# Feed-forward of a decoder layer: outputs of the down product with tokens on the partitions, operands exchanged, closing products in a tile of their own

## The chip, the core and the metric

The kernel runs on one core of one Trainium2 chip. A core has a matrix engine (TensorE, "PE" in the profile; its weight loads are listed apart as "PEld"), a vector engine (VectorE, "DVE"), a scalar engine (ScalarE, "ACT"), a general engine (GpSimd, "POOL") and a queue that only issues transfers (SyncE, "SP"). They run side by side and wait for one another through semaphores; 16 DMA engines move the data. SBUF is the working memory with 128 partitions. PSUM, which takes the results of TensorE, has eight banks, each of 512 fp32 per partition.

The metric is the time of one execution on the device, in microseconds (us). Lower is better.

## What is computed

The reference is one decoder layer on `x` of 8 sequences x 256 tokens x 512 features, all in fp32: self-attention, a recurrence that takes the place of cross-attention, and a gated feed-forward, each followed by an addition and a layer norm. Only the last one is touched here:

```python
gate_w = spline_reconstruct(gate_cp, INTER, HIDDEN)     # 2048 x 512
up_w   = spline_reconstruct(up_cp, INTER, HIDDEN)       # 2048 x 512
down_w = spline_reconstruct(down_cp, HIDDEN, INTER)     # 512 x 2048
gate  = jnp.einsum('bsh,ih->bsi', hidden_states, gate_w)
up    = jnp.einsum('bsh,ih->bsi', hidden_states, up_w)
inter = jax.nn.silu(gate) * up
return jnp.einsum('bsi,hi->bsh', inter, down_w)
...
x = _layernorm(x + _L0_ffn_ref(x, ...), axis=-1)
```

The weights are cubic splines through about 8,100 control points each, so most of a row is piecewise cubic. The kernel uses that: the down product is made of an exact part, 16 tiles of 128 intermediate features, of which each quarter of 32 is used for one quarter of the 512 outputs, and of a closing part, in which sums of intermediate features ("fin") stand for all that the exact part leaves out.

## The kernel before

The 2048 tokens are handled in four groups `b` of 512 tokens (`GT`), each of four chunks of 128 (`TC`). Attention comes first and fills the time up to about 402 us. From there the feed-forward runs group after group (loop at L939). Every instruction is issued in program order on its engine: the class `Ordered` (L299 to L312) pins the order that the Python code writes, so what stands earlier in the code stands earlier in each engine's queue. All instructions pass through that class and therefore carry its line, L308, in the profile; groups are told apart by the names of tiles.

One group, in the order of the code:

- `fill(DC)` (L942, groups 1 and 2 only) makes the transposes of the next group's input (`tr_x2`, four PSUM tiles of the pool `ps_mm`, which has four buffers in all). They are copied out alternately by ACT and DVE (L712).
- `gate_up(b, j)` for j = 0 to 7 (L842): two gate products `pg` (in `ps_mm`) and two up products `pu` (in `ps_big`, four buffers), ACT makes `sg = silu(pg)`, DVE `inter = pu * sg`. Right after each, `gather` (L858) sends both `inter` tiles by a transfer from SP's queue into `nat`, 256 KB each, 16 in a group. In groups 1 and 2 the moments of the next group's input (`ps_mom`) come after j = 2.
- `reads` (L953): transfers on SP's queue that bring the next group's input `xg` into place.
- `exact(b, t)` for t = 0 to 15 (L865): the exact down product, four matmuls per t, one for each output quarter d. The stationary operand is the weight `wd` (32 rows x 128 columns), the moving one `inter` (32 rows x 512 tokens). Result: `y0` to `y3`, four tiles of the pool `ps_big`, outputs on the partitions, tokens along the free axis. The four d sit in different 32-row strips of the array.
- After t = 7: the generator `residual(b)` (L920) is queued: POOL copies `x2` into `x2p` (36 copies, permuted features, each for all 512 tokens), handed out six at a time in the slots after t = 8 and later; and `into_sums(b, v)` for v = 0 to 3 (L875): products `ps_s` from `nat`, copied by ACT or DVE to `sum`, and sent by a transfer from POOL's queue into `fin` (`sorted_[b]`). POOL's four transfers stand ahead of its 36 copies.
- `finish(b)` (L894): four closing products (128 rows x 128 columns, 512 tokens moving) are added into `y0` to `y3` in PSUM, then each is copied to SBUF (`ys`), by ACT and DVE in turn.
- `outcome(b, t)` (L907), one generator for each chunk: four transposes `tr_y`, DVE adds `x2p` and sums up (`h3`, `s3`), and `norm_plain` (L366) makes the layer norm: DVE `nm`, ACT Square with sum, POOL `va` and `rs`, DVE the result; then SP sends it to `out`.

A generator in `chains` goes one step further at each call of `slot()`. The four `outcome` generators of group b - 1 are queued in the exact products of group b, behind t = 0 (L957), so their transposes stand between t = 0 and t = 1 of group b, and their transfers to `out` behind all gathers of group b on SP's queue. Those of the last group run behind everything (L973).

An fp32 matmul appears in the profile as two instructions ("passes"), each with its own weight load; a transpose as one.

## Time and profile before

| what | value |
|---|---|
| three runs | 602.85, 604.49, 605.11 us; median 604.49 |
| the profiled execution, its own time | 603.72 us |
| its span, first to last instruction | 601.9 us |
| mean granted clock of TensorE | 0.996 |
| feed-forward | 402.4 to 601.9 us |
| group 0: gates from, exact from, sums end, closing from | 402.4, 424.3, 439.9, 447.1 us |
| group 1 | 452.4, 470.1, 487.7, 495.6 us |
| group 2 | 500.9, 518.6, 536.2, 544.8 us |
| group 3 | 548.4, 562.3, 579.9, 587.1 us |

Group 0 has the last output projections and norms of attention between gates and exact products (416 to 424 us).

The profile names a group of instructions by what is written and read: `y<-inter,wd` are the exact products, `y<-fin,wd` the closing ones, `tr_y<-ident,ys` the transposes of the result, `x2p<-x` POOL's copies, `nat<-inter` the gathers. A line of the timeline has: start in us, length in us of the stretch of like instructions, engine, L308, operation, out<-in, rows*columns and sizes, count, and in brackets the engine's idle time before it with what ended it. Lengths of matmuls are modelled up to the arrival of the last result; the pace of the engine is read from start to start.

### The profile page before, as it was taken

To read this page: it belongs to the slowest core of one execution; us is meant where nothing else is said; L and a number is where in the kernel's file an instruction comes from. 1 tells how busy PE (TensorE), PEld (TensorE's weight loads), DVE (VectorE), ACT (ScalarE), POOL (GpSimd) and SP (SyncE) were. 2 spreads that over 40 slices of the span, in tenths; PEclk is the share of its full clock that TensorE was granted. 3 is DMA by queue.
4 is the path that set the end of the run, shared out by engine and by line. 5 is a ranking of instruction groups with operands and counts; after the bars stand their busy time and mean duration, and the time that the engine had idled before them with its cause. 6 is when DMAs were issued, how large, how long until landed. Compare 5 with 4: busy or idle time off the path is not lost.

```text
span 601.9 us, 9688 instructions
## 1 busy us (share of the span) xinstructions
PE 577.3 (96%) x3346; PEld 292.0 (49%) x3346; DVE 335.5 (56%) x742; ACT 277.9 (46%) x820; POOL 219.3 (36%) x495
## 2 busy tenths in 40 slices
PE   9999999998899999999999999999999999999993
PEld 4544555555455555554554555444444434433432
DVE  0203634658676665886674777776926605714614
ACT  0114643655654554655455667665315404504502
POOL 0000997065544336444340311300272262142244
PEclk9999999999999999999999999999999999999998
DMA  8104253034224115323210564659328986984931
GB/s 294 64 0 157 80 167 114 27 98 144 74 71 141 36 54 175 105 71 96 79 36 2 158 152 102 173 152 216 65 72 223 205 233 179 227 213 134 212 142 70
DMA packets 38961, 75.50 MB, mean 125 GB/s; under 512 B 3937, under 2 KB 8289, under 8 KB 38913
## 3 DMA queue, kind: packets, MB, share of 16 engines
q1 hardware_dynamic: 34576, 62.75, 39.4%
q0 software_dynamic: 3328, 10.96, 5.5%
q10 hardware_dynamic: 1008, 1.18, 0.7%
q8 instruction: 26, 0.43, 0.3%
q14 instruction: 23, 0.18, 0.1%
HBM read 42.86 MB, written 11.04 MB: 90 GB/s over the span
## 4 chain that ended last, share of the span: by engine, by line
PE 82%; DVE 10%; ACT 3%; DMA 2%; issue 2%; POOL 1%; POOLq 0%; DVEq 0%; SPq 0%; ACTq 0%
PE y L308 12%; PE ps_k L308 9%; PE ps_v L308 9%; PE ps_o L308 8%; PE ps_q L308 6%; PE tr_e L308 6%; PE sc L308 5%; PE pg L308 5%; PE ps_s L308 5%; PE av L308 5%; PE pu L308 5%; DVE nmax L308 3%; PE ps_mom L308 2%; ACT e L308 2%; DVE eT L308 2%
## 5 line engine op out<-in xcount | busy, mean ns | idle before, releaser
L308 ACT ACTIVATE e<-sc,nmax 128x256 f32<-128x256 f32 x256 | 120.2, 480 | 102.1 <-DVE nmax L308 102.1
L308 DVE TENSOR_REDUCE nmax<-sc 128x2 f32<-128x512 f32 x128 | 84.5, 682 | 73.6 <-PE sc L308 67.7
L308 POOL TENSOR_TENSOR taps<-taps 128x256 f32<-128x256 f32 (+1 forms) x144 | 89.0, 618 | 33.1 <-DMA taps<-in_down_taps 26.3
L308 PEld LDWEIGHTS tr_e<-ident,e 128*128 128x128 f32 x512 | 56.9, 140 | 25.2 <-issue 22.5
L308 PE MATMUL tr_e<-ident,e 128*128 128x128 f32 x512 | 68.3, 276 | 0.5 <-DVE eT L308 0.4
L308 PE MATMUL y<-inter,wd 32*128 32x512 f32 x512 | 63.0, 598 | 0.0
L308 PE MATMUL ps_o<-w_o,yT 128*128 128x512 f32 x128 | 60.0, 600 | 2.6 <-DVE eT L308 2.3
L308 PE MATMUL ps_k<-xT_g,w_k 128*128 128x512 f32 x128 | 58.8, 601 | 0.6 <-DVE eT L308 0.6
L308 PE MATMUL ps_v<-w_v,xT_g 128*128 128x512 f32 x128 | 58.6, 598 | 0.4 <-DVE eT L308 0.4
L308 PE MATMUL ps_q<-xT_g,w_q 128*128 128x512 f32 x128 | 58.2, 596 | 0.0
L308 POOL TENSOR_SCALAR va<-ss 128x1 f32<-128x1 f32 x32 | 7.3, 227 | 136.8 <-ACT x L308 86.6
L308 POOL TENSOR_TENSOR rs<-va,neghalf 128x1 f32<-128x1 f32 x48 | 28.9, 602 | 69.4 <-DVE va L308 66.7
L308 ACT ACTIVATION_READ_ACCUMULATOR e<-sc,nmax 128x1 f32 x256 | 53.2, 208 | 0.0
L308 DVE TENSOR_TENSOR inter<-pu,sg 128x512 f32<-128x512 f32 x64 | 41.2, 686 | 18.3 <-PE pu L308 9.4
L308 ACT ACTIVATE sg<-pg 128x512 f32<-128x512 f32 x64 | 37.2, 596 | 18.4 <-PE pg L308 18.4
L308 DVE COPY eT<-tr_e 128x512 f32<-128x512 f32 x64 | 43.8, 684 | 0.5 <-PE tr_e L308 0.4
L308 PEld LDWEIGHTS y<-inter,wd 32*128 32x128 f32 x512 | 26.7, 184 | 32.7 <-issue 27.0
L308 PE MATMUL av<-eT,v_g 128*32 128x256 f32 x512 | 36.7, 385 | 5.0 <-ACT eT L308 2.7
L308 ACT COPY eT<-tr_e 128x512 f32<-128x512 f32 x64 | 37.5, 585 | 2.4 <-PE tr_e L308 2.4
L308 POOL TENSOR_TENSOR r<-r 128x1024 f32<-128x1024 f32 x8 | 15.2, 1895 | 63.6 <-DMA r<-in_ctxT 63.6
L308 PE MATMUL sc<-k_g,q_g 32*128 32x256 f32 x512 | 37.4, 401 | 0.2 <-ACT e L308 0.2
L308 PEld LDWEIGHTS ps_o<-w_o,yT 128*128 128x128 f32 x128 | 22.8, 190 | 26.4 <-issue 21.5
(98 smaller groups left out, 737.5 us busy)
## 6 DMA issues: line engine op xcount, KB each, us to landing
nat<-inter SPq DMA_DIRECT2D x64, 256.0 KB
taps<-in_down_taps SPq DMA_DIRECT2D x40, 256.0 KB
taps<-in_up_taps SPq DMA_DIRECT2D x16, 384.0 KB
xg<-xd SPq DMA_DIRECT2D x8, 616.0 KB
r<-in_ctxT SPq DMA_DIRECT2D x8, 512.0 KB
x_t<-in_x SPq DMA_DIRECT2D x16, 256.0 KB
fin<-sum POOLq DMA_DIRECT2D x16, 256.0 KB, 5.1
out<-h SPq DMA_DIRECT2D x16, 256.0 KB
```

The costliest lines, as they stand in the source:

```text
L308: return lambda *a, **k: self.tc.keep_in_program_order(f(*a, **k))
```

## The change

The exact product exchanges its operands: `inter` (32 rows x 128 tokens of one chunk c) is now the stationary one, `wd` (32 rows x 128 outputs) the moving one. For each t there are 16 matmuls of 128 columns in place of four of 512, in the order c, then d. The result `y` has tokens on the partitions. It is one PSUM tile of four banks (bank d holds the four chunks of quarter d), of a new pool `ps_four` with a single buffer, opened when the attention's `ps_big` is closed. The four up products in flight are slices of a tile of the same tag ("big4"), so `y` of a group and `pu` of the next take turns in the same four banks.

The closing product is made apart, with exchanged operands too, per chunk, in a tile `ps_c` of `ps_mm` (16 matmuls of 128 columns in place of four of 512); it is no longer added in PSUM. DVE makes `h3 = y + x2p` from PSUM first and then `h3 = ps_c + h3` with the sum. The transposes `tr_y` and the copies `ys` are gone. Square's unused output goes to a tile `o` in SBUF.

The order changes as well: `finish(b)` issues the first two steps of all four `outcome` generators (the four additions of `y`, then closing products and second additions chunk by chunk), behind the last exact product of the same group. What is left of each, the norm and the transfer to `out`, is queued one chunk at a time behind j = 0, 1, 2, 3 of the next group's `gate_up` (`late_chains`).

```diff
-    ps_big = ctx.enter_context(tc.tile_pool(name="ps_big", bufs=4, space=PSUM))
     ps_mm = ctx.enter_context(tc.tile_pool(name="ps_mm", bufs=4, space=PSUM))
+    scored = ExitStack()
+    ps_big = scored.enter_context(tc.tile_pool(name="ps_big", bufs=4, space=PSUM))
...
+    scored.close()
+    ps_big = ctx.enter_context(tc.tile_pool(name="ps_four", bufs=1, space=PSUM))
...
     def gate_up(b, j):
         pgs, pus = [], []
-        for w, pool, tag, to in ((wg, ps_mm, "mm", pgs), (wu, ps_big, "big", pus)):
+        if not j:
+            ups[b] = ps_big.tile([P, 4, GT], F32, tag="big4", name="pu")
+        for w, to in ((wg, pgs), (wu, pus)):
             for h in range(2):
                 at = slice(h * K2, (h + 1) * K2)
-                ps = pool.tile([P, GT], F32, tag=tag, name="pg" if w is wg else "pu")
+                ps = ps_mm.tile([P, GT], F32, tag="mm", name="pg") if w is wg else ups[b][:, j % 2 * 2 + h, :]
...
     def exact(b, t):
         if t == 0:
-            ys[b] = [ps_big.tile([P, GT], F32, tag="big", name=f"y{d}") for d in range(ND)]
-        for d in range(ND):
-            q = slice(d * 32, (d + 1) * 32)
-            nc.tensor.matmul(
-                ys[b][d], lhsT=wd[q, t * P : (t + 1) * P], rhs=inters[b, t][q, :], start=(t == 0), stop=False
-            )
+            ys[b] = ps_big.tile([P, ND, TC, P], F32, tag="big4", name="y")
+        for c in range(TC):
+            for d in range(ND):
+                q = slice(d * 32, (d + 1) * 32)
+                nc.tensor.matmul(
+                    ys[b][:, d, c, :],
+                    lhsT=inters[b, t][q, c * P : (c + 1) * P],
+                    rhs=wd[q, t * P : (t + 1) * P],
+                    start=(t == 0 and c == 0),
+                    stop=(t == NTILE - 1 and c == TC - 1),
+                )
...
     def finish(b):
-        y = late.tile([P, ND, GT], F32, tag="ys", name="ys")
+        new = [outcome(b, c) for c in range(TC)]
+        for _ in range(2):
+            for chain in new:
+                next(chain)
+        late_chains.extend(new)
+
+    def outcome(b, c):
+        h3 = rows.tile([P, D], F32, tag="row", name="h3")
+        h, x2p = (a.rearrange("p (d o) -> p d o", d=ND) for a in (h3, xps[b][:, c, :]))
+        nc.vector.scalar_tensor_tensor(h, ys[b][:, :, c, :], 1.0, x2p, ALU.mult, ALU.add)
+        yield
+        acc = ps_mm.tile([P, D], F32, tag="mm", name="ps_c")
         for d in range(ND):
             nc.tensor.matmul(
-                ys[b][d],
-                lhsT=wd[:, (NTILE + d) * P : (NTILE + d + 1) * P],
-                rhs=sorted_[b][:, d, :],
-                start=False,
+                acc[:, d * P : (d + 1) * P],
+                lhsT=sorted_[b][:, d, c * P : (c + 1) * P],
+                rhs=wd[:, (NTILE + d) * P : (NTILE + d + 1) * P],
+                start=True,
                 stop=True,
             )
-            (nc.vector.tensor_copy if d % 2 else nc.scalar.copy)(y[:, d, :], ys[b][d])
-        ys[b] = y
-
-    def outcome(b, t):
-
-        tr = ps_mm.tile([P, D], F32, tag="mm", name="tr_y")
-        for d in range(ND):
-            nc.tensor.transpose(tr[:, d * P : (d + 1) * P], ys[b][:, d, t * P : (t + 1) * P], ident)
-        yield
-        h3 = rows.tile([P, D], F32, tag="row", name="h3")
         s3 = small.tile([P, 1], F32, tag="s3", name="s3")
-        nc.vector.scalar_tensor_tensor(h3, tr, 1.0, xps[b][:, t, :], ALU.mult, ALU.add, accum_out=s3)
-        yield from norm_plain(h3, s3, h3, tr)
-        r0 = (b * TC + t) * P
+        nc.vector.scalar_tensor_tensor(h3, acc, 1.0, h3, ALU.mult, ALU.add, accum_out=s3)
+        yield
+        o = work.tile([P, D], F32, tag="o", name="o", bufs=2)
+        yield from norm_plain(h3, s3, h3, o)
+        r0 = (b * TC + c) * P
         nc.sync.dma_start(out=out[r0 : r0 + P, :], in_=h3)
...
             if b:
+                if late_chains:
+                    chains.append(late_chains.pop(0))
                 slot()
...
             exact(b, t)
-            if b and t == 0:
-                chains += [outcome(b - 1, c) for c in range(TC)]
             slot()
...
         assert not units
+        settle()
         finish(b)
-    chains += [outcome(NG - 1, t) for t in range(TC)]
+    chains += late_chains
     settle()
```

More of the change, by code (lines that the diff above doesn't have):

```diff
@@ L839, in decoder_kernel @@
     made[0] = -1e9
-    inters, ys, sorted_, xps, nats = {}, {}, {}, {}, {}
+    inters, ys, sorted_, xps, nats, late_chains, ups = {}, {}, {}, {}, {}, [], {}
     def gate_up(b, j):
         pgs, pus = [], []
-        for w, pool, tag, to in ((wg, ps_mm, "mm", pgs), (wu, ps_big, "big", pus)):
+        if not j:
+            ups[b] = ps_big.tile([P, 4, GT], F32, tag="big4", name="pu")
+        for w, to in ((wg, pgs), (wu, pus)):
             for h in range(2):
                 at = slice(h * K2, (h + 1) * K2)
-                ps = pool.tile([P, GT], F32, tag=tag, name="pg" if w is wg else "pu")
+                ps = ps_mm.tile([P, GT], F32, tag="mm", name="pg") if w is wg else ups[b][:, j % 2 * 2 + h, :]
                 nc.tensor.matmul(ps, lhsT=w[at, j * P : (j + 1) * P], rhs=xgs[b][at, j, :], start=True, stop=True)
@@ L894, in finish @@
     def finish(b):
-        y = late.tile([P, ND, GT], F32, tag="ys", name="ys")
+        new = [outcome(b, c) for c in range(TC)]
[9 more added lines that the diff above has]
+        acc = ps_mm.tile([P, D], F32, tag="mm", name="ps_c")
         for d in range(ND):
             nc.tensor.matmul(
-                ys[b][d],
-                lhsT=wd[:, (NTILE + d) * P : (NTILE + d + 1) * P],
-                rhs=sorted_[b][:, d, :],
-                start=False,
+                acc[:, d * P : (d + 1) * P],
+                lhsT=sorted_[b][:, d, c * P : (c + 1) * P],
+                rhs=wd[:, (NTILE + d) * P : (NTILE + d + 1) * P],
+                start=True,
                 stop=True,
             )
-            (nc.vector.tensor_copy if d % 2 else nc.scalar.copy)(y[:, d, :], ys[b][d])
-        ys[b] = y
-    def outcome(b, t):
-        tr = ps_mm.tile([P, D], F32, tag="mm", name="tr_y")
-        for d in range(ND):
-            nc.tensor.transpose(tr[:, d * P : (d + 1) * P], ys[b][:, d, t * P : (t + 1) * P], ident)
-        yield
-        h3 = rows.tile([P, D], F32, tag="row", name="h3")
-        s3 = small.tile([P, 1], F32, tag="s3", name="s3")
-        nc.vector.scalar_tensor_tensor(h3, tr, 1.0, xps[b][:, t, :], ALU.mult, ALU.add, accum_out=s3)
-        yield from norm_plain(h3, s3, h3, tr)
-        r0 = (b * TC + t) * P
+        s3 = small.tile([P, 1], F32, tag="s3", name="s3")
+        nc.vector.scalar_tensor_tensor(h3, acc, 1.0, h3, ALU.mult, ALU.add, accum_out=s3)
+        yield
+        o = work.tile([P, D], F32, tag="o", name="o", bufs=2)
+        yield from norm_plain(h3, s3, h3, o)
+        r0 = (b * TC + c) * P
         nc.sync.dma_start(out=out[r0 : r0 + P, :], in_=h3)
```

## The prediction

> **What bounds the kernel now.** I read the page first, then the timeline of the last group, whose order all groups share, then the stretches around it for the transfers.

> ```profile
> PE 577.3 (96%) x3346; PEld 292.0 (49%) x3346; DVE 335.5 (56%) x742; ACT 277.9 (46%) x820; POOL 219.3 (36%) x495
> ...
> PE 82%; DVE 10%; ACT 3%; DMA 2%; issue 2%; POOL 1%; POOLq 0%; DVEq 0%; SPq 0%; ACTq 0%
> ```

> TensorE is busy 96% of the span and holds 82% of the chain that ends last. So work taken from it counts, as long as nothing else is close behind. The next two views ask what is close behind in the feed-forward.

> ```profile
> 564.84 1.97 PE L308 MATMUL tr_y<-ident,ys 128*128 128x128 f32 x16
> ...
> 566.74 6.29 PE L308 MATMUL y<-inter,wd 32*128 32x512 f32 x56
> ...
> 572.96 7.09 PE L308 MATMUL ps_s<-nat,sf 128*64 128x512 f32 x32
> ...
> 579.97 7.15 PE L308 MATMUL y<-inter,wd 32*128 32x512 f32 x64
> 580.09 0.69 DVE L308 COPY sum<-ps_s 128x512 f32<-128x512 f32 x1 [2.74 <-PE ps_s L308]
> ...
> 581.08 0.55 POOL L308 DMA_DIRECT2D fin<-sum  x1 [1.28 <-DVE sum L308]
> ...
> 581.62 8.18 POOL L308 COPY x2p<-x 128x4 f32<-128x4 f32 x36
> ...
> 587.05 3.70 PE L308 MATMUL y<-fin,wd 128*128 128x512 f32 x8
> ...
> 592.97 0.69 ACT L308 ACTIVATE tr_y<-h,nm 128x512 f32<-128x512 f32 x1 [2.45 <-DVE nm L308]
> ```

> TensorE goes from the transposes through exact products, sums, exact products and closing without a hole. But POOL's copies to `x2p` end at 589.8, 2.8 us after the last exact product (587.0). They can't start sooner: POOL first issues the four `fin` transfers, and the last waits for DVE's copy of the last sum. Counting from S, the end of the sums (579.9), `x2p` is complete at S+9.9. The copies of all four groups end at S+9.9 (449.8, 497.6, 546.1, 589.8). Today that hurts nobody, since `x2p` is read only behind the transposes.

> ```profile
> 552.00:556.00 4.00, 4.00 (x22) 1.83 (x20) 3.00 (x5) 2.76 (x5) 0.00 (x0) 1.00 0.92 210
> 556.00:560.00 4.00, 4.00 (x20) 1.74 (x18) 3.14 (x6) 2.54 (x5) 0.00 (x0) 1.00 1.08 214
> ...
> 568.00:572.00 4.00, 4.00 (x42) 1.85 (x38) 3.00 (x8) 1.84 (x6) 2.90 (x7) 1.00 1.08 207
> 572.00:575.00 3.00, 3.00 (x22) 0.97 (x16) 0.00 (x0) 0.06 (x1) 0.00 (x0) 1.00 0.95 343
> ```

> The last two columns are the DMA engines' share and GB/s. From 552 to 572 the engines are full at some 211 GB/s: 20 us x 0.211 = 4.2 MB, the 16 gathers of 0.262 MB. Behind them, at 343 GB/s, go the four `out` transfers, which today stand behind all gathers on SP's queue. The last gather's semaphore comes at 572.5. The first sum product that reads it starts at 573.8 (0.86 behind 572.96). So the gathers are only 1.3 us from being the bound.

> **The change, part by part.** Times are relative to G, the start of a group's gates, and to S.

> Exact products. Before, a t takes two passes of 512 columns at 0.429 us from start to start, 0.858 us, the four strips side by side. After, eight passes of 128 columns, each with a weight load of 128 columns in all strips. Nearest rows: `tr_y`, 16 passes of 128 columns with a load each at 0.108 us from start to start; and the full-height fp32 product `ps_wq`, 0.112. So 0.86 to 0.89 us; I take 0.88, +0.2 per half group. This needs 64 instructions per t in 0.88 us, 13.7 ns each. The trace shows no such pace for long: its densest 64 PE instructions (67.64 to 69.41, score products and transposes) come at 27.7 ns. That end is a rival below. I take the fast end, because the loads of the four strips of `y` start within 0.02 us of each other.

> [...]

> First exact product. It needs all four banks that `pu` held, so it waits for the last `inter`; today it already does (470.15 to 472.61 for one t), so 0.

> Transposes. Three times between t = 0 and t = 1: 1.90 plus one change of shape, 0.09: -1.99 each. The fourth set is in the tail.

> Closing. 32 passes at 0.112 = 3.57 us in place of 3.43. What hides the 0.14 is DVE's chain, next.

> The new wait. DVE's first addition reads `x2p` straight behind the exact products, so it starts at S+9.95, not at S+7.3. Then four additions at 0.60 from start to start (as `inter`, same form) and four second additions at 0.74 (`h<-tr_y` less its `nm`): starts at S+12.35, 13.1, 13.8, 14.6. Each `ps_c` buffer of `ps_mm` comes free some 0.7 later, and behind these wait, on TensorE, the next group's transposes and gates. Closing products are done by S+12.6 even where `fin` lands at S+8.5 (groups 1 and 2), so DVE sets the time. Groups 0 and 1: `tr_x` of the second chunk must be copied by DVE behind its last second addition, S+15.3 to 16.0, before `pg` has its two buffers: gates start at S+16.1. Before: 452.43 - 439.88 = 12.55, and 500.91 - 487.74 = 13.15: +3.55 and +2.95. Group 2 has no `tr_x`: two `ps_c` buffers free at S+13.85, before 548.35 - 536.22 = 12.15: +1.7. Last group: the first Square waits for `nm` behind all second additions, S+15.6; before 592.97 - 579.88 = 13.1: +2.5; from there on the rows are as now (4.84 to the last result). `y` is free at S+12.6, before `pu` needs it.

> The moved transfers. The four `out` of a group now go out behind j = 3 to 6 of the next group (two of them in the pause for the moments), ahead of the last two gathers on SP's queue. 1.05 MB at 343 GB/s and 0.95 share: 2.9 us later for the last gather. Below 0 it can't go; at the gathers' rate it would be 5 us. I take 2.9, measured on these very transfers. Group 3: last gather at 572.5 - 548.35 = G+24.15, now G+27.05; its first reader was at G+25.45: +1.6, in place of the -1.8 that TensorE would gain. Groups 1 and 2: packets through at G+25.9, semaphore some 0.4 later, now G+29.2; reader before at G+29.25: 0, in place of -1.8. Moments and `xg` on these queues come later but have 2 us to spare.

> The norms beside the gates: ACT gets a Square each at 0.81, 1.99 for 1.72 us of TensorE at j = 1 to 4; up to 1 us late, and the gathers hide it.

> Sum: group 0 exact +0.2; into group 1 +3.55; group 1 0; into 2 +2.95; group 2 0; into 3 +1.7; group 3 +1.6; tail +2.5. Together +12.5 against the profiled execution's 603.7 (span 601.9 and 1.8 around it): 616.2. The median stands 0.8 above that execution, inside the runs' scatter, so I say 616.

> One more risk: in group 3 TensorE idles about 3.4 us before the last gather. After the last matmul (593.1) the granted clock holds at 0.99 to 596.8 and reads 0.50 behind that; a hole of 2.0 us at 158.6 left it at 1.00. So 3.4 us should just pass; else up to 2 us more, which the range holds.

> [...]

> **Rivals.** (1) The `out` transfers slip between the gathers without delaying them. For: they are written while DMA also waits for `inter`; against: the share is 0.92 and up. Then groups 1 and 2 gain 1.8 each and group 3 1.3: 616.2 - 1.8 - 1.8 - 2.9 = 609.7. (2) The issue of PE instructions becomes the bound at 27.7 ns: 1.77 us per t, +7.3 per half. Group 0 +7.1; the second halves end at S+14.4 and push DVE by 4.6, four times, 18.4; first halves of groups 1 to 3 beyond the gathers 5.4, 5.4 and 3.7: 616.2 + 40 = 656. Against: nothing in the trace is held up by issue for long. (3) `x2p` is not waited for: POOL would have to be done by S+7.1. Gates then lose only 0.85, 0.2 and 0.1 and the tail gains 0.2: +0.2 + 0.95 + 1.6 = 606.4, no measurable change. (4) Faster: TensorE alone stays the bound, at the boundaries and at the sums. It decides where the copies are done by S+7.1 and the gathers by G+23.6. Then three times -1.99, exact +1.4, boundaries and tail +0.95: 600.1. For: 96% busy; against: both margins above, 2.8 and 1.3 us, read from the trace.

> **How the numbers follow.** Forecast 0.64, (1) 0.15, (2) 0.08, (3) 0.07, (4) 0.06. The time is the forecast's, 616. The range, 606 to 624, holds the forecast with its bounds (`out` at the slow rate 6 more in all, the clock 2), (1) and (3), and leaves out (2) and (4). Within 0.5% of 604.5 is 601.5 to 607.5, about what runs of this kernel can tell from no change: faster 0.06, same 0.07, slower 0.87.

> **What would show it.** Right: `tr_y` gone; exact products at 0.86 to 0.89 us per t; DVE idle before the first addition with POOL's `x2p` as releaser, in all four groups; `ps_s` or its second product waiting for the transfer `nat` in group 3; holes on TensorE of 2 to 4 us at each boundary. Wrong: exact products well above 1 us per t; additions that start right behind the exact products; sums that start 1.8 us sooner after G in every group.

## The result, and the profile after

The changed kernel takes 642.0 us (641.33 to 643.1), beside 604.8 for the kernel before on the same chip: ratio 1.0616, 95% interval 1.0595 to 1.0637. The forecast was 616 us, range 606 to 624: the sign was right, the size was not.

The profiled execution took 643.1 us, its span is 641.3. Starts of first instructions, read from the timeline as for the table of before, give the loss by stage. S is the end of the sums, and the last column holds the next group's first gate product, or the end of the span.

| group | gates to sums, before and after | sums | S to next gates or end | loss |
|---|---|---|---|---|
| 0 | 30.55, 36.93 | 6.93, 6.93 | 12.55, 16.03 | 9.9 |
| 1 | 28.39, 38.41 | 6.92, 9.27 | 13.17, 15.45 | 14.7 |
| 2 | 28.39, 32.51 | 6.92, 6.92 | 12.13, 15.92 | 7.9 |
| 3 | 24.61, 29.53 | 6.92, 6.92 | 22.02, 23.88 | 6.8 |

With 0.2 us ahead of 402 us this makes the 39.4 us by which the span grew. The forecast had put 10.7 us of its 12.5 into the fourth column. That column holds 11.4 us of the 39.4; 25.4 lie between gates and sums. The page of the changed kernel says where to look (busy time, the DMA queue of instructions, and three groups with, behind the last bar, TensorE's or DVE's idle time ahead of them):

```profile
PE 584.4 (91%) x4914; PEld 328.5 (51%) x4914; DVE 337.0 (53%) x750; ACT 272.0 (42%) x812; POOL 218.0 (34%) x495
...
q8 instruction: 39, 0.64, 0.4%
...
L308 PE MATMUL y<-wd,inter 32*128 32x128 f32 x2048 | 63.7, 278 | 11.6 <-issue 7.2
...
L308 DVE TENSOR_TENSOR inter<-pu,sg 128x512 f32<-128x512 f32 x64 | 41.2, 686 | 36.7 <-ACT sg L308 23.0
...
L308 PE MATMUL pu<-xg,wu 64*128 64x512 f32 x128 | 36.0, 634 | 15.6 <-DVE inter L308 11.5
```

TensorE is busy 7 us longer than before, not 39. Two waits are new and were in no part of the forecast: up products wait for `inter`, and exact products wait for "issue", which means for nothing that the profile shows. The timeline of group 0's gates shows the first.

```profile
404.69 1.29 DVE L308 TENSOR_TENSOR inter<-pu,sg 128x512 f32<-128x512 f32 x2 [0.82 <-ACT sg L308]
...
406.03 1.13 PE L308 MATMUL pu<-xg,wu 64*128 64x512 f32 x4 [0.59 <-DVE inter L308]
...
407.28 1.29 DVE L308 TENSOR_TENSOR inter<-pu,sg 128x512 f32<-128x512 f32 x2 [1.30 <-PE pu L308]
...
408.62 1.13 PE L308 MATMUL pu<-xg,wu 64*128 64x512 f32 x4 [0.60 <-DVE inter L308]
```

The up products of each j start when DVE has read those of j - 1, and DVE in turn waits for them. One j takes 408.62 - 406.03 = 2.59 us. In the kernel before (here in group 3) it took 557.90 - 556.18 = 1.72, and no up product waited for DVE:

```profile
556.18 1.02 PE L308 MATMUL pu<-xg,wu 64*128 64x512 f32 x4
...
557.29 1.29 DVE L308 TENSOR_TENSOR inter<-pu,sg 128x512 f32<-128x512 f32 x2 [0.43 <-ACT sg L308]
...
557.90 1.02 PE L308 MATMUL pu<-xg,wu 64*128 64x512 f32 x4
```

The up products alternate between two pairs of banks, so the data leave room for two j at a time, but all four banks are one tile. Gates and up products together take 20.0 to 23.9 us in place of 13.9 to 17.6.

The second wait lies in the exact products. This is group 1 in the timeline, and then the same stretch by windows (busy time and count of PE, PEld, DVE, ACT and POOL, then TensorE's granted clock, DMA share and GB/s).

```profile
489.75 5.20 PE L308 MATMUL y<-wd,inter 32*128 32x128 f32 x179
489.77 5.03 SPq L308 DMA_DIRECT2D xg<-xd  x3
...
499.54 1.43 PE L308 MATMUL y<-wd,inter 32*128 32x128 f32 x17 [4.60 <-issue]
```

```profile
494.00:497.00 3.00, 0.94 (x35) 0.75 (x27) 0.00 (x0) 0.00 (x0) 0.00 (x0) 1.00 0.75 148
497.00:500.70 3.70, 1.16 (x17) 1.14 (x17) 0.00 (x0) 0.00 (x0) 0.00 (x0) 0.75 0.73 158
500.70:503.00 2.30, 2.30 (x11) 0.77 (x8) 0.00 (x0) 0.00 (x0) 0.00 (x0) 0.50 0.66 175
503.00:506.00 3.00, 3.00 (x10) 0.83 (x8) 0.00 (x0) 0.59 (x1) 0.49 (x1) 0.56 0.60 135
```

In the middle of products whose data have long been there, TensorE stops for nearly 5 us, with no engine at work and no releaser. Transfers are under way (the gate inputs `xg` of group 2). Afterwards the granted clock is 0.50 (the half clock), and the sums of this group take 9.27 us in place of 6.92. A hole of 2.90 us lies in the second half of group 2 (569.84), again with the half clock behind it (0.50 from 574.0 to 576.9 us).

What the forecast was mostly about did come. This is the view of the tile `x2p` (what ended DVE's idle time before it read the tile, us and times):

```profile
L308 DVE SCALAR_TENSOR_TENSOR h<-y,x2p x16: 680/681/692, 456.4 to 629.2; 128x512 f32<-128x512 f32 x16
its engine sat idle before it (us, times) until:
  POOL x2p L308: 27.2, 3
  PE y L308: 11.3, 1
```

In three groups DVE waits for POOL's copies, as forecast in all four. In group 2 the copies were done first (574.9 us), since its exact products ran into the hole at 569.84.

### The profile page after: what moved, and what is told of

Its sections match the earlier page's. It is cut to its first block, busy times and chain, and to the rows that moved or that the text cites. A ratio compares the mean times of both kernels' runs of the same rounds, so it can differ in the third digit from the quotient of the medians.

```text
span 641.3 us, 12808 instructions
## 1 busy us (share of the span) xinstructions
PE 584.4 (91%) x4914; PEld 328.5 (51%) x4914; DVE 337.0 (53%) x750; ACT 272.0 (42%) x812; POOL 218.0 (34%) x495
## 5 line engine op out<-in xcount | busy, mean ns | idle before, releaser
L308 ACT ACTIVATE e<-sc,nmax 128x256 f32<-128x256 f32 x256 | 120.0, 479 | 102.0 <-DVE nmax L308 102.0
L308 DVE TENSOR_REDUCE nmax<-sc 128x2 f32<-128x512 f32 x128 | 84.5, 682 | 73.6 <-PE sc L308 67.7
L308 POOL TENSOR_TENSOR taps<-taps 128x256 f32<-128x256 f32 (+1 forms) x144 | 89.1, 619 | 32.7 <-DMA taps<-in_down_taps 24.6
L308 PE MATMUL y<-wd,inter 32*128 32x128 f32 x2048 | 63.7, 278 | 11.6 <-issue 7.2
L308 PEld LDWEIGHTS y<-wd,inter 32*128 32x128 f32 x2048 | 60.9, 191 | 19.2 <-issue 11.6
L308 PEld LDWEIGHTS tr_e<-ident,e 128*128 128x128 f32 x512 | 56.9, 141 | 25.2 <-issue 22.5
L308 PE MATMUL tr_e<-ident,e 128*128 128x128 f32 x512 | 68.3, 276 | 0.6 <-DVE eT L308 0.4
L308 PE MATMUL ps_o<-w_o,yT 128*128 128x512 f32 x128 | 60.0, 600 | 2.4 <-DVE eT L308 2.1
L308 DVE TENSOR_TENSOR inter<-pu,sg 128x512 f32<-128x512 f32 x64 | 41.2, 686 | 36.7 <-ACT sg L308 23.0
L308 PE MATMUL ps_k<-xT_g,w_k 128*128 128x512 f32 x128 | 59.3, 605 | 0.5 <-DVE eT L308 0.5
L308 PE MATMUL ps_v<-w_v,xT_g 128*128 128x512 f32 x128 | 58.6, 598 | 0.4 <-DVE eT L308 0.4
L308 PE MATMUL ps_q<-xT_g,w_q 128*128 128x512 f32 x128 | 58.2, 596 | 0.0
L308 ACT ACTIVATE sg<-pg 128x512 f32<-128x512 f32 x64 | 37.4, 596 | 47.1 <-PE pg L308 46.8
L308 ACT ACTIVATION_READ_ACCUMULATOR e<-sc,nmax 128x1 f32 x256 | 53.2, 208 | 0.0
L308 POOL TENSOR_TENSOR rs<-va,neghalf 128x1 f32<-128x1 f32 x48 | 27.7, 577 | 70.1 <-DVE va L308 67.4
L308 POOL TENSOR_SCALAR va<-ss 128x1 f32<-128x1 f32 x32 | 7.0, 218 | 129.8 <-ACT x L308 92.3
L308 PE MATMUL pu<-xg,wu 64*128 64x512 f32 x128 | 36.0, 634 | 15.6 <-DVE inter L308 11.5
L308 DVE COPY eT<-tr_e 128x512 f32<-128x512 f32 x64 | 43.7, 683 | 0.5 <-PE tr_e L308 0.4
L308 PE MATMUL av<-eT,v_g 128*32 128x256 f32 x512 | 36.7, 385 | 5.0 <-ACT eT L308 2.7
L308 ACT COPY eT<-tr_e 128x512 f32<-128x512 f32 x64 | 37.4, 585 | 2.4 <-PE tr_e L308 2.4
L308 PE MATMUL sc<-k_g,q_g 32*128 32x256 f32 x512 | 37.4, 401 | 0.2 <-ACT e L308 0.2
L308 POOL TENSOR_TENSOR r<-r 128x1024 f32<-128x1024 f32 x8 | 15.2, 1895 | 64.2 <-DMA r<-in_ctxT 64.2
```

Source lines behind the costliest of these rows:

```text
L308: return lambda *a, **k: self.tc.keep_in_program_order(f(*a, **k))
```

## The experiments

The theories behind the expectations: A, the shared tile makes the up products wait; C, TensorE's instructions come in blocks, and the blocks come late; E, the copies to `x2p` hold up the boundary. B, D, F and G are rivals, told in the expectations (the letter F stands for one rival in the third run and for another in the test with four pieces). Times of the kernel before on the chips of these runs were 603.2 to 604.0 us; an edit is against the changed kernel where nothing else is said.

### The shared tile

First run (624 us): the up products are four tiles of a pool of their own, opened for each group and closed before the tile `y` takes the banks.

```diff
+            banks(f"ps_pu{b}", 4)
-                ps = ... ups[b][:, j % 2 * 2 + h, :]
+                ps = ... four["pool"].tile([P, GT], F32, tag="big", name="pu")
...
+            banks(f"ps_y{b}", 1)
```

> Undoes one part of the change: the up products are four tiles of a pool of their own again, opened and closed per group, in the same four banks as y. Theory A (the slices of one tile make each pair of up products wait for DVE's read of the pair before, in other banks): gates go back from 2.59 to 1.72 us per j, 13.8 us in groups 0 and 3; 24 us less from that, of which 2 to 6 come back where the sums then wait for the last gather: 618 to 624 us. Rival B (the norms, now beside the gates, hold ACT and DVE up): the waits stay in groups 1 to 3, and at most group 0's 6 us go: 636 us or more.

Measured: 624.29 us, ratio 1.0334 (1.0292 to 1.0376). Gates and up products are back at 13.85, 17.93, 17.93 and 14.06 us. B falls. The time lies 0.3 us above A's range; the exact products now have four holes (1.73, 2.79, 2.90 and 3.93 us) in place of two (4.87 and 2.90).

The other direction, the kernel before with this one part alone, operands and everything else as they were:

```diff
+            ups[b] = banks(f"ps_pu{b}", 1).tile([P, 4, GT], F32, tag="big4", name="pu")
...
-                ps = pool.tile([P, GT], F32, tag=tag, ...)
+                ps = ps_mm.tile(...) if w is wg else ups[b][:, j % 2 * 2 + h, :]
```

> The kernel before with one part of the change alone: each group's up products are slices of one tile of four banks (the banks are handed on to y's four tiles behind the gates, as in the first experiment); operands, transposes, copies and finish are those of before. Theory A (the up products of j wait for the last read of the up products of j - 1, though these lie in other banks): 2.59 us per j in place of 1.72, gates 5 to 6 us longer in each of the four groups, no holes in the exact products: 624 to 629 us. Rival (the slower gates of the changed kernel come from what runs beside them there, the norms, the moved out transfers or the order of the pools): under 612 us.

Measured: 628.03 us, ratio 1.0416 (1.0398 to 1.0435). Its timeline of group 0:

```profile
405.31 1.13 PE L308 MATMUL pu<-xg,wu 64*128 64x512 f32 x4 [0.59 <-DVE inter L308]
...
406.56 1.29 DVE L308 TENSOR_TENSOR inter<-pu,sg 128x512 f32<-128x512 f32 x2 [1.30 <-PE pu L308]
...
407.90 1.13 PE L308 MATMUL pu<-xg,wu 64*128 64x512 f32 x4 [0.60 <-DVE inter L308]
```

Again 2.59 us per j and the same two waits as in the changed kernel, with nothing else changed, and no hole in the exact products. So this part alone costs 24.8 us on the kernel before. Taken back from the changed kernel it gives 17.7 only, since four holes then stand where there were two. I read that as the transfers' doing: with slow gates more of them are through before the exact products start.

### The holes in the exact products

Where do the holes sit? I counted the records on TensorE's queue (matmuls, weight loads, and the hundred or so semaphore and drain instructions between them) from the start of the program up to each hole of more than 0.9 us between two exact products. The last number is what is left when the count is divided by 256:

```
kernel                    hole at us (length)   records before it, modulo 256
changed kernel            494.67 (4.87)         6593, 193
                          569.84 (2.90)         8385, 193
up products as four tiles 480.51 (1.73)         6593, 193
                          530.59 (2.79)         7873, 193
                          548.48 (2.90)         8385, 193
                          581.12 (3.93)         9153, 193
```

The changed kernel and seven of the experiments have 26 such holes, and all 26 stand at 193 modulo 256. (Matmuls and weight loads alone, without the semaphore and drain instructions, give no common place.) The page's queue of instructions moved 0.64 MB in 39 packets, 16.4 KB each, beside 9927 records on TensorE's queue; in the feed-forward one packet comes for about every 256 instructions of TensorE (22 packets from 402.48 to 626.56 us, 5330 records from the first to the last, 254 for each step). Where few transfers run, a packet mostly starts 10 to 60 records behind such a place and takes about 1 us; I read it as the fetch of a block ahead. In group 1 of the changed kernel the place before was passed at about 491.1 us, the next fetch started at 496.53, 5.4 us behind it, and took 1.25; TensorE had run dry at 494.67 and was back at 499.54. The DMA view from 490 to 496.4 us has the data queue alone (packets, MB, share); the one from 496.4 to 499 has the one packet of instructions:

```profile
q1 hardware_dynamic: 624, 1.16, 84.7%
...
q1 hardware_dynamic: 231, 0.43, 70.0%
q8 instruction: 1, 0.02, 3.0%
```

It is the same at all 26 holes: the last fetch started 1.9 to 5.4 us behind the place before, took 1.0 to 1.4, and TensorE was back 1.2 to 1.8 us after its end. Why it starts late beside transfers the traces don't show; the tests below show only on what it depends. In the kernel before the fetches of the feed-forward lie 17 to 29 us apart; its exact products use up a block in 13.7 (16 instructions in 0.858 us), and no hole of more than 0.9 us lies between them. The exact products of the changed one use up a block in 3.6 (256 x 14.0 ns).

The second run of the first set left out half of the gathers (those of t from 8 on; the sums read the first half's tile twice).

```diff
-        nc.sync.dma_start(out=nats[b, g][r::NSUM], in_=inters[b, t])
+        if not g:
+            nc.sync.dma_start(out=nats[b, g][r::NSUM], in_=inters[b, t])
```

> The changed kernel with only the gathers of t = 0 to 7; the sums read these tiles in place of the others, so TensorE's work is the same and the sums are of other numbers. Theory C (TensorE's instruction blocks, read through the DMA engines, come late while the gathers fill these): no hole over 0.5 us inside the exact products, sums of group 1 in 6.9 us and not 9.3, granted clock 1.00 there: 8 to 10 us less, 632 to 634. Rival D (TensorE's own issue can't keep 14 ns per instruction): holes and clock as before, 640 to 643.

Measured: 639.52 us, ratio 1.0573 (1.0529 to 1.0617). That lies just below rival D's range and far above C's, so this run decides nothing. The hole of group 2 shrank from 2.90 to 0.83 us; that of group 1 stayed, 4.20 us, beside the reads of `xg`, which this kernel still makes. So I made a test that changes only the number of instructions, and another that takes away all the transfers.

The kernel before, its operands and finish untouched, with exact products in four pieces of 128 tokens:

```diff
-        for d in range(ND):
+        for c, d in [(c, d) for c in range(4) for d in range(ND)]:
...
-                ys[b][d], ..., rhs=inters[b, t][q, :], start=(t == 0), ...
+                ys[b][d][:, at], ..., rhs=inters[b, t][q, at], start=(t == 0 and c == 0), ...
```

> The kernel before, with each exact product of 512 tokens made in four pieces of 128: the operands keep their roles, the transposes and the old finish stay, and TensorE gets as many instructions as in the changed kernel (64 per t). Theory C (instruction blocks of 256 come late while the DMA queues are full; at 13.9 ns per instruction a block lasts only 3.5 us): holes of 2 to 5 us in the exact products of groups 1 to 3, each at the same place in the count of TensorE's instructions modulo 256, the half clock behind the long ones, 612 to 622 us. Rival F (the exchange of the roles itself makes the holes, as tokens are then the weights that are loaded): no holes, 0.2 to 0.4 us more per half, 604 to 607 us.

Measured: 618.42 us, ratio 1.0249 (1.0209 to 1.0288). Its timeline and windows in group 1:

```profile
484.95 1.01 PE L308 MATMUL y<-inter,wd 32*128 32x128 f32 x9 [4.40 <-issue]
```

```profile
480.30:485.00 4.70, 0.30 (x15) 0.11 (x7) 0.00 (x0) 0.00 (x0) 0.00 (x0) 0.82 0.83 190
485.00:489.00 4.00, 4.00 (x17) 1.67 (x19) 0.00 (x0) 0.00 (x0) 0.00 (x0) 0.50 0.85 198
```

Holes of 4.67, 1.12, 3.40 and 2.75 us, all at 193 modulo 256, and the half clock behind the first and the last (0.50 from 485 to 489 us, 0.54 from 585.5 to 588). Rival F falls: the exchange of the roles isn't needed for the holes, the number of instructions is enough. The same with two pieces of 256 (`range(2)`):

> The same with two pieces of 256: 32 instructions per t, a block lasts about 7 us. Theory C: a fetch that starts 5.5 us late, takes 1.25 us and is in use 1.7 us later (sizes from the hole at 494.7 us of the changed kernel) needs 8.5 us, so holes of at most 1.5 us each, three or four of them: 604 to 608 us, and none that brings the half clock. A rival in which a fixed time is lost per block under load, however fast it is used up, would have holes as long as with four pieces: 610 us and more.

Measured: 604.62 us, ratio 1.002 (1.0003 to 1.0037), no hole over 0.9 us between exact products. With 32 instructions per t a block lasts 6.9 us, and no late fetch shows as a hole. Halving the density of instructions takes away 13.8 of 15.2 us.

Next, all of the changed kernel's work on TensorE, with four tiles for the up products, and without the transfers beside it: from group 1 on the gathers, in groups 2 and 3 the reads of the gate inputs.

```diff
+        if b:
+            nats[b, g] = nats[0, g]
+            return
...
-        xg = pool.tile(...)
+        xg = xgs[b - 2] if b > 1 else pool.tile(...)
```

> The changed kernel with the up products as four tiles, as in the first experiment, and without the transfers that run beside exact products: from group 1 on the gathers are left out (the sums read group 0's), and groups 2 and 3 read no gate inputs of their own (they use those of groups 0 and 1). TensorE's work is all there. Theory C: no hole over 0.5 us in the exact products, clock 1.00 throughout, some 15 us less than the first experiment's 624: 606 to 612 us. Rival G (TensorE's own sequencer can't keep 14 ns for more than some 500 instructions): the holes stay, 620 us or more.

Measured: 609.02 us, ratio 1.0081 (1.0056 to 1.0106). Windows over the first halves of groups 1, 2 and 3:

```profile
473.50:481.00 7.50, 7.46 (x258) 7.35 (x260) 0.00 (x0) 0.00 (x0) 0.00 (x0) 1.00 0.05 19
...
522.80:530.20 7.40, 7.37 (x258) 7.25 (x258) 0.00 (x0) 0.00 (x0) 0.00 (x0) 1.00 0.05 18
567.80:575.20 7.40, 7.35 (x256) 7.24 (x256) 0.00 (x0) 0.00 (x0) 0.00 (x0) 1.00 0.06 22
```

With a DMA share of 0.05 to 0.06 there is no hole and, in these windows, no half clock: 512 instructions in 7.16 us at a time. Rivals D and G fall: TensorE keeps this pace if its instructions are there.

The positive test puts 16 transfers more (the second half of group 0's `inter` tiles, twice, into DRAM) beside the exact products of group 0, which had no hole in any kernel so far.

```diff
+        if not b:
+            spare = ffn["dram"].tile([16, P, GT], F32, tag="spare", name="spare")
+            for i in range(16):
+                nc.sync.dma_start(out=spare[i], in_=inters[0, 8 + i % 8])
```

> The changed kernel with the up products as four tiles, and 16 transfers of 0.262 MB more from SBUF to DRAM, queued behind group 0's gathers, so that they run beside group 0's exact products, which had no hole in any run so far. Theory C: one to three holes of 1.5 to 5 us in group 0's exact products, at the same place modulo 256 as the others; 628 to 636 us. Rival G: group 0 stays without holes, 622 to 627 us.

Measured: 622.62 us, ratio 1.0314 (1.028 to 1.0349). Windows in group 0:

```profile
429.20:430.30 1.10, 0.36 (x13) 0.17 (x7) 1.03 (x6) 0.00 (x0) 0.55 (x1) 1.00 1.05 400
```

A hole of 1.01 us appears at 429.28, record 5057, 193 modulo 256. The place is as C has it. The size is below what I expected, and the total lies in rival G's range (622 to 627), so it is the hole and its place that speak for C here, not the time. These transfers move 400 GB/s, the gathers some 210: a full queue alone doesn't say how late a fetch will be.

### The boundaries

The third run of the first set queues POOL's copies to `x2p` ahead of the exact products (in group 0 behind t = 4, when their buffer exists), and so ahead of the sums.

```diff
+        if b:
+            chains.append(residual(b))
         for t in range(NTILE):
             exact(b, t)
...
             if t == 7:
                 settle()
-                chains.append(residual(b))
```

> The changed kernel with POOL's copies to x2p queued at the start of the exact products (group 0: behind t = 4) in place of behind the sums. Theory E (the additions wait for these copies at each boundary): first addition right behind the last exact product, boundaries shorter by 2.3 to 2.7 us in groups 0 and 1 and in the tail, group 2 depends on where the exact products stall: 634 to 637. Rival F (PSUM buffers and DVE's own chain of eight additions set the boundary): 1 us or less in all, 641 or more.

Measured: 637.86 us, ratio 1.0527 (1.0454 to 1.06). From S to the next gates: 13.6 us behind groups 1 and 2 (15.45 and 15.92 in the changed kernel), so E holds there; the end of the kernel came 2.3 us sooner too, and rival F (1 us or less in all) falls. The time is 0.9 us above E's range. Behind group 0 it became 17.6 (16.03): the copies now stood ahead of the transfers to `fin` on POOL's queue, and the closing products waited for these until 455.63.

The fourth run joined the four tiles, the early copies, and the norms and `out` transfers moved back behind the next group's first exact product (where the kernel before has them).

> Both edits, and the norms with their transfers to out behind the next group's first exact product, as before the change. If A, C and E hold, the gates' 24 us, the boundaries' 8 and the out transfers' delay of the gathers go, and the exact products' late instruction blocks stay: 604 to 612 us. If nothing but the forecast's parts were left and instruction blocks came in time: 600.

Measured: 624.43 us, ratio 1.0325 (1.0276 to 1.0374): a clear miss. Gates and boundaries gained, and the exact products lost it again: holes of 4.54, 3.35, 3.02 and 4.37 us, with the half clock behind all but the third (means of 0.58, 0.50 and 0.64 over stretches behind these, 1.00 behind the third). This run showed me that the holes, not the waits, were what was left to explain.

Two more with the copies of groups 1 to 3 early and group 0 left alone, one on the quiet kernel above (which leaves the same transfers out), one whole:

> The quiet kernel (up products as four tiles; from group 1 on the gathers, and in groups 2 and 3 the reads of the gate inputs, left out) with POOL's copies to x2p of groups 1 to 3 queued ahead of the exact products. It shows what the change would bring without the shared tile, the late blocks and the wait for x2p in groups 1 to 3. From the quiet kernel's 609: 1.9 us less between the sums of group 1 and the gates of group 2 (15.5 to 13.6, the value that the copies gave in the third experiment), 0 to 1 less in group 2, 1.9 to 2.5 less in the tail: 603.5 to 605.5, so no gain over the kernel before even then. If the waits for x2p alone had stood between the change and a gain, the boundaries would fall to the 12.2 to 13.2 of before and the time to 600 or less.

> The whole computation, with the up products as four tiles and the copies to x2p of groups 1 to 3 queued ahead of the exact products: the best form of the change that the runs so far point to. From 624 and 622.6 for the four tiles alone less 3.5 to 5 us at two boundaries and the tail: 618 to 621, still slower than before by 15 us or more, the late blocks being all there.

Measured: 607.75 us, ratio 1.0074 (1.0052 to 1.0095), and 621.71, ratio 1.0273 (1.0236 to 1.0309; one of its four executions took 1489.68 us, which I can't explain; the median of the other three is 621.08, at the upper edge of what was expected). The first missed by 2 us, and the timeline of its group 3 says why, beside the same instruction in the quiet kernel:

```profile
562.14 8.39 POOL L308 COPY x2p<-x 128x4 f32<-128x4 f32 x36
...
564.41 2.16 DVE L308 TENSOR_SCALAR h<-h,nm,rs 128x512 f32<-128x512 f32 x1
566.49 1.27 DVE L308 TENSOR_TENSOR inter<-pu,sg 128x512 f32<-128x512 f32 x2
...
567.82 3.43 PE L308 MATMUL y<-wd,inter 32*128 32x128 f32 x64 [3.34 <-DVE inter L308]
```

```profile
566.05 0.54 DVE L308 TENSOR_SCALAR h<-h,nm,rs 128x512 f32<-128x512 f32 x1
```

Beside POOL's copies the last step of a norm takes DVE 2.16 us in place of 0.54 (1.73 and 1.77 in groups 1 and 2). The last `inter` stands behind it on DVE, and the first exact product behind that: TensorE idles 3.3 us and then gets the half clock (a mean of 0.57 from 568 to 572 us), so the first half takes 8.78 us in place of 7.16 (in group 1 too). In groups 1 and 2 the first exact product also comes 1.1 and 1.2 us later after the first gate than in the quiet kernel. In group 3 it doesn't (567.82 against 567.85), since there the quiet kernel has the half clock on its gates: 0.50 from 552 to 554 us, behind the wait at the boundary, 2.0 us lost. The copies' gain at the boundaries and the end, 6.2 us in all, is mostly given back in these places.

No kernel here beats the one before. The quiet kernel is a bound for the idea as it stands: without the shared tile, without late blocks and without a wait for gathers it is still 5.8 us slower (609.02 against 603.24).

## Why the prediction was wrong

Two steps failed, both by a cost that was set to nothing.

**"`y` is free at S+12.6, before `pu` needs it."** Beside the wait of the first exact product for the last `inter`, this was all that the forecast said of the new tile for the up products, and it looked only at the tile's first use in a group. It never asked what the slices do to each other from j to j + 1. Alone on the kernel before they cost 24.8 us, about twice the 12.5 that the forecast had added up in all; taken back from the changed kernel they gave 17.7. The diff showed the cause: four tiles became one, and the loop writes a slice of it that DVE isn't reading while DVE reads another.

**The exact products "by pace".** The pace was about right: 0.894 us per t where the forecast had 0.86 to 0.89 and took 0.88, so 14.0 ns per instruction over 512. The forecast weighed whether TensorE can issue that fast, and set the rival at 27.7 ns against it ("nothing in the trace is held up by issue for long"); that rival is refuted by the quiet kernel's 7.16 us per half. What neither asked is whether instructions arrive that fast. With half as many per t nothing is lost (604.62), with the full number 15.2 us are (618.42, roles as before), and in the changed kernel with four tiles 15.3 go when the transfers beside it go (624.29 to 609.02). The line that could have raised the question was on the page of before: a DMA queue of instructions (`q8 instruction: 26, 0.43, 0.3%`).

The rest, by the forecast's steps:

- First exact product, 0: borne out. In group 1 it starts at 487.97, right behind the last `inter` (487.91), and its t takes 0.9 us; before, the first t started sooner but was stretched over 2.46 us by the same wait.
- Transposes, -1.99 each, with the sums no earlier because of the gathers: the transposes went, but the gathers were not the bound. From the end of the last `inter` to the sums, groups 2 and 3 took 7.85 us in place of 9.22. In the view of `nat` no product waits for it in the changed kernel, nor in the first run; slower gates or late blocks gave the gathers time. So the 2.9 us of the moved `out` transfers can't be seen, and what they would cost behind fast gates without holes was not tried.
- The new wait for `x2p`: borne out, its size within some 0.7 us. The copies ended at S+9.9 in all four groups, DVE started straight behind them in three, and the gates of group 1 began at S+16.0 (forecast 16.1). Group 2's came at 15.5 (16.1), those of group 3 at 15.9 (13.85), where the 2.90 us hole came first; in the quiet kernel, without it, they came at 13.1. The tail lost 1.9 us (2.5).
- Closing products, hidden: they were done by 457.75 us behind group 0, and DVE's additions set the gates at 462.5.
- The norms beside the gates, hidden: with four tiles the gates of groups 1 and 2 took 17.93 us in place of 17.63, those of group 3 14.06 in place of 13.85, so nearly.
- The clock: the forecast let a hole of 3.4 us pass. Holes of 2.6 to 2.9 us mostly brought the half clock already (below), and so did the wait at a boundary in the quiet kernel (above). The forecast's 2 us for a halved clock was an estimate of mine that no row of the kernel before shows; what the runs showed is 2.35 us more for the sums of group 1 in the changed kernel (9.27 for 6.92) and 2.0 us on the gates of group 3 in the quiet one.

Put beside the forecast's own sum: without the shared tile, the holes and the gathers' delay, its rival (1) gives 609.7 us, and the quiet kernel, which has none of these, measured 609.02. That the two agree so closely is partly luck. Rival (1) has +10.7 us at the boundaries and the end and -4.7 from gates to sums; the quiet kernel's profile, beside that of the kernel before, has +8.0 and -2.3. The errors of 2.7 and 2.4 us cancel, and 2.0 of the second are the half clock on group 3's gates, which the forecast left out. So the terms that were worked out were right to some 3 us; the two that were set to nothing held the rest: 17.7 and 15.3 us, taken away one after the other.

## What to carry to other kernels

When tiles are merged into slices of one, ask for every pair of a write and a read of different slices whether a wait now stands between them, and cost the loop with it; here it turned a loop of 1.72 us into one of 2.59. When a change multiplies TensorE's instructions, work out how long a block of 256 lasts at their pace and hold the time against how late a fetch can be beside the transfers that run there: 7 us per block was safe in this kernel (604.62 us, no hole), 3.6 was not (618.42, four holes). A gain behind a wait is worth what the next wait leaves of it, so a change with several parts is worth running part by part.
